# Projection weights' loads begun by ScalarE instead of SyncE, with new places for the work

## The chip, the cores and the metric

The kernel runs on one core of a Trainium2 chip. The metric is the device time of one execution in microseconds; 1185.76 us is the median of three runs of the kernel before. A profiled execution gives, beside the time, a record of every instruction and transfer: TensorE (PE, with its weight loads as PEld), VectorE (DVE), ScalarE (ACT), GpSimd (POOL) and SyncE (SP), which here only starts DMA transfers.

## The reference

One layer over 8 sequences of 256 tokens with 256 features, all in float32. The input is normalized; an attention with 16 heads and a feed-forward part both read the normalized input, and both are added to the input.

```python
xn = _layernorm(x)
q, k = rope(xn @ Wq.T), rope(xn @ Wk.T)            # 16 heads of 128
v, g = xn @ Wv.T, xn @ Wg.T
s = clip(xn @ Ws1.T @ Ws2.T + bs2, -32, 32)        # 64 slots a head
es, enz = exp(s), exp(-cumlogsumexp(s))            # over the tokens
ok = enz * (tril(q @ k.T * scale) @ es)
qv = softmax(ok)
o = tril((qv * enz) @ es.T) @ v
attn = (rmsnorm(o) * g_norm_weight * silu(g)) @ Wo.T
inter = gelu(xn @ Wgate.T) * (xn @ Wup.T)          # 2048 wide, weights from 4-bit codes and scales
out = x + attn + inter @ Wdown.T
```

## The kernel before, in words

The tokens are cut into four groups of 512 (two sequences each), the heads into eight pairs. The attention runs over 32 steps, one for each group and pair of heads; the feed-forward part is cut into small units that are put between the attention's. The program is written out by a planner at build time (`manual_schedule`): it keeps a clock for each engine, estimates when the stages of a chain can run, and so decides in which order the instructions stand in each engine's queue. On the chip each queue runs strictly in that order; semaphores hold an instruction back until its inputs are there.

A loop step n holds the units of several attention steps. `POS` gives each unit's place within the loop step, from 0 to 1; `START` gives other places for the first two loop steps; `FEED` says over which part of a loop step the feed-forward units are spread, `FIRST`, `LAST` how many of them the first and last loop steps get, `DUE` how many pieces of feed-forward weights are to be decoded by each step, and `NORM_AT` where the later groups' normalizations are begun. Where a unit's inputs would be late by the planner's clock, it puts in up to four feed-forward units ahead of it.

The units of an attention step, in the order of the data:

- `rope` (four for a step: q and k of two heads, L637): two matmuls of 512 columns into a bank (L645); ScalarE copies the bank's halves crosswise (L655, L656); VectorE multiplies by the cosines (L658); GpSimd multiplies by the sines and adds (L663, L664).
- `states` (L573): two small matmuls (L584), the clipping (L598), exponentials (L602, L619), prefix sums (L624) and four reciprocals (L630), which make `enz`; `es` is turned by a transposition of blocks (L519), four stores to DRAM (L523), a load back (L532) and a copy (L612).
- `value` and `gate` (two each, L670 and L683, matmuls L706): v is copied (L679), the gate is made of a tanh (L692) and a product (L694).
- `scores` (two, L718): q by k (L725, L728), masked by VectorE (L716).
- `logits` (L736): matmuls L745, product with `enz` (L756), and the way through DRAM as for `es`, to `okT`.
- `softmax` (L769): maxima (L781), exponentials (L792), the same way through DRAM again, and GpSimd's product that makes `prT` (L803).
- `cross` (L811), `weights` (L835, matmuls L845, masked by L855) and `apply` (L872), in the loop step after.
- `outputs` (two, L879, matmuls L888), the normalization and gating (L901, L906, L910, L914), the way through DRAM, and `close` (L929, matmuls L941), which adds two steps' heads to the residual.

The feed-forward units are `ffn_gate` (L437 with L444, L446, L448, L450, L452), `ffn_up` (L466, L475) and `ffn_down` (L491, L409). Their weights are decoded by VectorE (L388, L392, L394). The eight PSUM banks are given out in the order in which the planner expects them to come free; a matmul into a bank waits for the last reader of its former content.

A step's projection weights lie in two tiles, one for q and k (`wts0`) and one for v and the gate (`wts2`), with one buffer each. So a load of the next step's weights must wait until the last matmul has read the old ones. All transfers are started by SyncE, whose queue runs in order: what stands behind a load that waits, waits too. `load_w` (L254) starts a load, and has places of its own, behind the fourth `rope` and the fourth `vg` unit of a loop step:

```python
put("rope", 3, load_w, n + 2, 0)
...
put("vg", 3, load_w, n + 1, 2)
```

Of the kernel before, what the change touches and what calls it, by code (L numbers as in the profile page):

```python
# [34 lines left out]

POS = {'scores': (0.054, 0.064),
 'logits': (0.148,),
 'softmax': (0.335,),
 'cross': (0.146,),
 'weights': (0.169,),  # L40
 'low': (0.1465,),
 'states': (0.167,),
 'outputs': (0.364, 0.453),
 'close': (0.367, 0.61),
 'rope': (0.176, 0.315, 0.368, 0.485),
 'vg': (0.561, 0.79, 0.922, 0.953)}
START = {-1: {'states': (0.575,), 'rope': (0.155, 0.358, 0.421, 0.588)},
 0: {'vg': (0.044, 0.057, 0.103, 0.241),
     'scores': (0.082, 0.162),
     'states': (0.336,),  # L50
     'logits': (0.251,),
     'softmax': (0.433,),
     'rope': (0.238, 0.267, 0.272, 0.485)}}
FEED = {-1: (0.336, 1.0)}
NORMS = {0: 1, 2: 2, 5: 3}
WO = (1, 3, 4, 6)
NORM_AT = (0.204, 0.593)
FIRST = [0.17, 1.57]
LAST = [1.56, 3.5]
DUE = [4, 6, 7, 7, 8, 9, 10, 11, 11, 11, 12, 13, 14, 15, 16, 16, 16, 16, 18, 19, 19, 22, 23, 23, 24]  # L60


@with_exitstack
def layer_kernel(ctx: ExitStack, tc: tile.TileContext, a: dict, out: bass.AP):
# [15 lines left out]
    nc = tc.nc  # L80
# [21 lines left out]
    def V(n):  # L102
        return "v", 0.15 + 0.00105 * n
# [4 lines left out]
    def pe(t):  # L108

        clock["pe"] += t  # L110
# [12 lines left out]
    def advance(until=None):  # L123

        while chains:
            c = min(chains, key=lambda c: (begin(c), c.rank))
            t = begin(c)
            if until is not None and t > until:
                return
            if isinstance(c.what, Chain):  # L130
                c.at = t
            else:
                e, cost, *kb = c.what
                clock[e] = t + cost
                c.at = t + cost + 0.1
                if kb:
                    c.at = lands(clock[e], kb[0])
            c.what = next(c.gen, None)
            if c.what is None:
                chains.remove(c)  # L140
                for users in c.banks:
                    if not any(u in chains for u in users):
                        freed.append(max(u.at for u in users))
            if until is None:
                return
# [4 lines left out]
    asking = [False]  # L150
# [85 lines left out]
    wts = {}  # L236
# [17 lines left out]
    def load_w(n, k):  # L254

        if n < N:
            w = aw.tile([P, 2, 2, 2 * DK], F32, tag=f"wts{k}", name=f"wts{k}")
            nc.sync.dma_start(out=w, in_=a["wqkvg"][steps[n][1]][:, k : k + 2])
            wts[n, k] = w
            loads((n, k), 512)  # L260

# [311 lines left out]
    def states(n):  # L573
# [60 lines left out]
        to["es_at"] = chain(swapped(), es, u)  # L634
        to["states"] = chain(summed(), esT, enz)

    def rope(n, j, which):  # L637

        g, hp = steps[n]
        w = wts[n, 0][:, which, :, j * DK : (j + 1) * DK]  # L640
        need_x(g)
        clock["pe"] = max(clock["pe"], landed[n, 0])
        ps = bank()
        for c in range(2):
            nc.tensor.matmul(  # L645
                ps, lhsT=w[:, c, :], rhs=xT[:, c, g * G : (g + 1) * G], start=c == 0, stop=c == 1
            )
        tag = "qk"[which]
        y = new(p2, [P, 2, T], tag, 2)
        z = new(p2, [P, 2, T], "z", 2)  # L650
        pv = ps.rearrange("p (b t) -> p b t", b=2)

        def work():
            yield "s", 1.16
            nc.scalar.copy(z[0:64], pv[64:128])  # L655
            nc.scalar.copy(z[64:128], pv[0:64])  # L656
            yield V(512)
            nc.vector.tensor_tensor(y, pv, cos_b, ALU.mult)  # L658

        def added():  # L660
            yield first
            yield "g", 2.55
            nc.gpsimd.tensor_tensor(z, z, sin_b, ALU.mult)  # L663
            nc.gpsimd.tensor_tensor(y, y, z, ALU.add)  # L664

        pe(1.72)
        first = chain(work(), ps, y, z)
        of[n][tag, j] = y, chain(added(), y, z)

# [13 lines left out]
    def gate(n, i):  # L683

        to = of[n]
        if i == 0:
            to["sg"] = new(p2, [P, TC, 2 * DK], "sgate")
        s, (pst, ps) = to["sg"][:, i : i + 2, :], vg(n, 1, i)

        def work():  # L690
            yield S(512)
            nc.scalar.activation(s, ps, AF.Tanh, scale=0.5)  # L692
            yield V(512)
            nc.vector.scalar_tensor_tensor(s, s, 1.0, ps, ALU.add, ALU.mult)  # L694

        to["sg", i] = chain(work(), pst, to["sg"])

    def vg(n, which, i):
        g, w = steps[n][0], wts[n, 2]
        need_x(g)  # L700
        pst = bank()
        ps = pst.rearrange("p (i d) -> p i d", i=2)
        for k in range(2):
            tt = slice(g * G + (i + k) * P, g * G + (i + k + 1) * P)
            for c in range(2):
                nc.tensor.matmul(  # L706
                    ps[:, k, :], lhsT=xT[:, c, tt], rhs=w[:, which, c, :],
                    start=c == 0, stop=c == 1,
                )
        pe(1.72)  # L710
        return pst, ps
# [291 lines left out]
    for n in range(-1, N + 1):  # L1003
        at = []
        pos = START.get(n, {})

        def put(name, k, f, *args):
            place = pos.get(name, POS[name])
            at.append((place[k], len(at), f, args))

        def put_at(place, f, *args):
            at.append((place, len(at), f, args))

        def put_norm(g, places):
            for k, h in enumerate((0, 2)):
                put_at(places[k], norm, g, h)

        if n == -1:
            put_norm(0, (0.0, 0.0))
            for h in (0, 2):  # L1020
                put_at(0.1, norm_turn, 0, h)
            put_at(0.2, low_rank, 0)
        if n + 1 < N:
            if n >= 0 and steps[n][1] == 7:
                put("low", 0, low_rank, steps[n][0] + 1)
            put("states", 0, states, n + 1)
            for k, (j, which) in enumerate(((0, 0), (0, 1), (1, 0), (1, 1))):
                put("rope", k, rope, n + 1, j, which)
            put("rope", 3, load_w, n + 2, 0)
        if 0 <= n < N:  # L1030
            for k, (f, i) in enumerate(((value, 0), (value, 2), (gate, 0), (gate, 2))):
                put("vg", k, f, n, i)
            put("vg", 3, load_w, n + 1, 2)
            for j in range(2):
                put("scores", j, scores, n, j)
            put("logits", 0, logits, n)
            put("softmax", 0, softmax, n)
        if n in WO:
            put_at(0.6, load_wo, 4 * WO.index(n))
        gn = NORMS.get(n)  # L1040
        if gn:
            if gn > 1:
                put_at(0.0, load_x, gn * TC, TC)
            put_norm(gn, NORM_AT)
        if n > 0:
            put("cross", 0, cross, n - 1)
            put("weights", 0, weights, n - 1)
            for k in range(2):
                put("outputs", k, outputs, n - 1, k)
            if n % 2 == 1 and n > 1:  # L1050
                for k in range(2):
                    put("close", k, close, n - 2, 2 * k)
            if n == N:
                for k in range(2):
                    put_at(2.0, close, N - 1, 2 * k)
        upto = round(banks * sum(weight[: n + 2]) / sum(weight))
        lo, hi = FEED.get(n, (0.0, 1.0))
        for k in range(upto - fed):
            put_at(lo + (hi - lo) * (k + 0.5) / (upto - fed), feed)
        fed = upto  # L1060
        upto = DUE[n + 1] if n + 1 < len(DUE) else 24
        for k in range(sent, upto):
            put_at((k - sent + 0.3) / (upto - sent), lambda k=k: k < len(parts) or decode_next())
        sent = max(sent, upto)
        for _, _, f, args in sorted(at, key=lambda e: e[:2]):
            while f is close and args == (N - 1, 2) and feeding:
                last, *its = feeding.pop(0)
                last(*its)
            if f is feed:
                ahead = ahead - 1 if ahead > 0 or not feed() else ahead  # L1070
                continue
            while f in UNITS and not ready(f, args):
                if ahead >= AHEAD and n < N or not feed():
                    f(*args)
                    break
                ahead += 1
            if f not in UNITS:
                f(*args)
            advance(clock["pe"])
            while ahead < 0 and feed():  # L1080
                ahead += 1
# [74 lines left out]
```

## Time and profile before

| | |
|---|---|
| median of three runs | 1185.76 us (1185.39 to 1186.27) |
| profiled execution | 1186.14 us |
| its span | 1184.4 us |
| mean granted TensorE clock | 0.997 |
| weight loads (L258) | 64 of 512 KB, median 3.8 us to landing |

The page gives the busy time of each engine as a share of the span. An engine's idle time is put down to what ended it, with total, number and longest of the waits. In timelines a row has its start, its length, the engine, the line, and in brackets the idle time ahead of it. Times count from the span's start.

### The profile page before, as it was taken

How to read it: one execution, taken by the hardware profiler on the slowest of the kernel's cores; microseconds unless marked ns; L12 is line 12 of the kernel's file. 1: busy time of each engine (PE TensorE's matmuls, PEld its weight loads, DVE VectorE, ACT ScalarE, POOL GpSimd, SP SyncE). 2: the span in 40 equal slices, each digit the busy share in tenths (PEclk: the TensorE clock that was granted, in tenths of full speed). 3: DMA queues.
4: the chain of work that ended last, by engine and by line, in shares of the span. 5: the costliest groups of instructions: out<-in, count | busy, mean ns of one | idle time of the engine just before them, and what ended most of it. 6: DMA issues, size and time to landing. Idle time of an engine off the chain costs nothing.

```text
span 1184.4 us, 18121 instructions
## 1 busy us (share of the span) xinstructions
PE 1173.3 (99%) x5830; PEld 828.5 (70%) x5830; DVE 881.3 (74%) x1690; ACT 537.3 (45%) x1685; POOL 490.7 (41%) x439
## 2 busy tenths in 40 slices
PE   9899999999999999999999999999999999999998
PEld 6466676866767777767767677676676677766865
DVE  7978878886676788877587776868777666768553
ACT  4544444554444454443454543535544344555321
POOL 5445435454343444443354443444434334454110
PEclk9999999999999999999999999999999999999999
DMA  5335444454343443343343334334333433432322
GB/s 209 111 106 165 136 124 148 134 143 120 89 134 99 116 135 97 96 117 109 90 143 116 99 112 121 109 106 125 92 97 106 117 103 111 135 98 79 106 58 61
DMA packets 143087, 135.30 MB, mean 114 GB/s; under 512 B 21264, under 2 KB 110480, under 8 KB 142992
## 3 DMA queue, kind: packets, MB, share of 16 engines
q1 hardware_dynamic: 142992, 134.15, 38.7%
q8 instruction: 46, 0.75, 0.3%
q14 instruction: 49, 0.40, 0.1%
HBM read 88.47 MB, written 45.61 MB: 113 GB/s over the span
## 4 chain that ended last, share of the span: by engine, by line
PE 87%; DVE 6%; DMA 2%; SPq 2%; issue 1%; POOL 1%; ACT 1%; DVEq 0%; ACTq 0%; POOLq 0%
PE ps L645 17%; PE ps L706 16%; PE ps L491 9%; PE ps L941 9%; PE ps L466 8%; PE ps L437 8%; PE ps L888 4%; PE ps L725 4%; PE ps L745 3%; PE ps L845 3%; PE ps L728 2%; PE ps L584 1%; PE ps L820 1%; DMA okT<-by_way 1%; SPq L523 1%
## 5 line engine op out<-in xcount | busy, mean ns | idle before, releaser
L663 POOL TENSOR_TENSOR z<-z,turns 128x512 f32<-128x512 f32 x128 | 169.6, 1325 | 226.8 <-ACT z L656 220.7
L645 PE MATMUL ps<-xT,wts 128*128 128x512 f32 x512 | 240.3, 599 | 0.5 <-ACT xT L349 0.5
L706 PEld LDWEIGHTS ps<-wts,xT 128*128 128x128 f32 x1024 | 194.5, 190 | 61.4 <-issue 32.5
L706 PE MATMUL ps<-wts,xT 128*128 128x256 f32 x1024 | 236.5, 379 | 0.0
L645 PEld LDWEIGHTS ps<-xT,wts 128*128 128x128 f32 x512 | 91.0, 190 | 82.9 <-issue 74.8
L437 PE MATMUL ps<-xT,w_gate 128*128 128x512 f32 x256 | 120.8, 594 | 0.2 <-DVE at L716 0.2
L466 PE MATMUL ps<-xT,w_up 128*128 128x512 f32 x256 | 120.7, 594 | 0.0
L630 DVE RECIPROCAL enz<-enz 128x128 f32<-128x128 f32 x128 | 118.4, 933 | 0.0
L491 PE MATMUL ps<-w_down,inter 128*128 128x256 f32 x512 | 115.7, 380 | 0.0
L941 PE MATMUL ps<-w_o,ogT 128*128 128x256 f32 x496 | 112.1, 379 | 0.0
L655 ACT COPY z<-ps 64x512 f32<-64x512 f32 x128 | 74.5, 582 | 82.3 <-PE ps L645 67.3
L491 PEld LDWEIGHTS ps<-w_down,inter 128*128 128x128 f32 x512 | 96.3, 190 | 16.3 <-issue 4.0
L446 POOL TENSOR_SCALAR t<-t 128x512 f32<-128x512 f32 x64 | 39.7, 621 | 150.3 <-ACT t L444 147.7
L803 POOL TENSOR_TENSOR prT<-okT,enz 128x512 f32<-128x512 f32 x32 | 40.6, 1269 | 148.2 <-DMA okT<-by_way 141.8
L941 PEld LDWEIGHTS ps<-w_o,ogT 128*128 128x128 f32 x496 | 93.1, 190 | 12.5 <-issue 0.5
L664 POOL TENSOR_TENSOR q<-q,z 128x512 f32<-128x512 f32 x64 | 84.1, 1315 | 34.3 <-DVE q L658 31.0
L664 POOL TENSOR_TENSOR k<-k,z 128x512 f32<-128x512 f32 x64 | 82.1, 1282 | 30.8 <-DVE k L658 13.2
L409 DVE TENSOR_TENSOR res<-ps,res 128x512 f32<-128x512 f32 x63 | 42.6, 679 | 68.9 <-PE ps L491 42.4
L910 POOL TENSOR_TENSOR ss<-ss,nhalf 128x4 f32<-128x4 f32 x64 | 65.6, 1025 | 59.8 <-DVE ss L906 59.0
L792 ACT ACTIVATE ok<-okT,mx 128x64 f32<-128x64 f32 x256 | 85.6, 337 | 10.0 <-DVE mx L786 9.3
L444 ACT ACTIVATE t<-ps 128x512 f32<-128x512 f32 x64 | 38.1, 596 | 109.2 <-PE ps L437 109.1
L448 DVE TENSOR_TENSOR t<-ps,t 128x512 f32<-128x512 f32 x64 | 43.4, 680 | 58.2 <-POOL t L446 58.0
(83 smaller groups left out, 1934.3 us busy)
## 6 DMA issues: line engine op xcount, KB each, us to landing
wts<-in_wqkvg_dram SPq DMA_DIRECT2D x64, 512.0 KB, 3.8
by_way<-ok SPq DMA_DIRECT2D x256, 64.0 KB, 1.8
okT<-by_way SPq DMA_DIRECT2D x64, 256.0 KB, 2.8
by_way<-og SPq DMA_DIRECT2D x256, 64.0 KB, 1.8
ogT<-by_way SPq DMA_DIRECT2D x64, 256.0 KB, 2.9
by_way<-u SPq DMA_DIRECT2D x128, 64.0 KB, 1.8
u<-by_way SPq DMA_DIRECT2D x32, 256.0 KB, 2.8
pk<-in_codes_dram SPq DMA_DIRECT2D x12, 256.0 KB, 3.7
```

Source lines behind the costliest of these rows:

```text
L437: nc.tensor.matmul(pg, lhsT=w_gate[:, c, ns], rhs=xT[:, c, gs], start=c == 0, stop=c == 1)
L466: nc.tensor.matmul(pu, lhsT=w_up[:, c, ns], rhs=xT[:, c, gs], start=c == 0, stop=c == 1)
L491: nc.tensor.matmul(ps[:, k, :], lhsT=inter[g, n][0][:, (i + k) * P : (i + k + 1) * P], rhs=w_dn[:, n, :], start=n == 2 * q, stop=n == 2 * ...
L630: nc.vector.reciprocal(r, r)
L645: nc.tensor.matmul(ps, lhsT=w[:, c, :], rhs=xT[:, c, g * G : (g + 1) * G], start=c == 0, stop=c == 1)
L655: nc.scalar.copy(z[0:64], pv[64:128])
L663: nc.gpsimd.tensor_tensor(z, z, sin_b, ALU.mult)
L664: nc.gpsimd.tensor_tensor(y, y, z, ALU.add)
L706: nc.tensor.matmul(ps[:, k, :], lhsT=xT[:, c, tt], rhs=w[:, which, c, :], start=c == 0, stop=c == 1,)
L792: nc.scalar.activation(pr[:, js, i, :], okT[:, js, i, :], AF.Exp, bias=mx[:, k : k + 1], scale=SCALE, accum_out=sm[:, k : k + 1],)
L910: nc.gpsimd.tensor_tensor(ss, ss, nhalf, ALU.pow)
L941: nc.tensor.matmul(ps[:, k, :], lhsT=ogT[hh][0][:, i + k], rhs=w_o[:, (hp // 2) * 4 + hh, :], start=hh == 0, stop=hh == 3,)
```

## The change

The loads for the first two steps stay where they were. From the third step on a load is started by ScalarE, in the middle of the stages of the last unit that reads the old weights: behind the second crosswise copy of the fourth `rope` for q and k, and behind the tanh of the second `gate` unit for v and the gate. As a load is now begun by a stage of a chain, and not by a unit, the new function `given` makes the planner advance its chains until the load has been begun, before a unit reads the new tile. Places of `softmax`, `outputs`, `close`, `rope` and `vg` are changed, and several for the first two loop steps; the shares of feed-forward units in the first and last loop steps, one place of the normalizations and two entries of `DUE` are changed too.

```diff
- 'softmax': (0.335,),
+ 'softmax': (0.267,),
- 'outputs': (0.364, 0.453),
- 'close': (0.367, 0.61),
- 'rope': (0.176, 0.315, 0.368, 0.485),
- 'vg': (0.561, 0.79, 0.922, 0.953)}
-START = {-1: {'states': (0.575,), 'rope': (0.155, 0.358, 0.421, 0.588)},
+ 'outputs': (0.307, 0.396),
+ 'close': (0.433, 0.61),
+ 'rope': (0.179, 0.318, 0.371, 0.488),
+ 'vg': (0.622, 0.79, 0.922, 0.953)}
+START = {-1: {'states': (0.575,), 'rope': (0.155, 0.358, 0.421, 0.543)},
-     'states': (0.336,),
-     'logits': (0.251,),
-     'softmax': (0.433,),
+     'states': (0.262,),
+     'logits': (0.241,),
+     'softmax': (0.437,),
-FEED = {-1: (0.336, 1.0)}
+FEED = {-1: (0.156, 1.0)}
-NORM_AT = (0.204, 0.593)
-FIRST = [0.17, 1.57]
-LAST = [1.56, 3.5]
-DUE = [4, 6, 7, 7, 8, 9, 10, 11, 11, 11, 12, 13, 14, 15, 16, 16, 16, 16, 18, 19, 19, 22, 23, 23, 24]
+NORM_AT = (0.291, 0.593)
+FIRST = [0.06, 1.57]
+LAST = [1.53, 3.5]
+DUE = [4, 6, 7, 7, 8, 9, 10, 11, 11, 11, 12, 13, 14, 15, 16, 16, 16, 16, 18, 18, 19, 22, 23, 24, 24]
...
-            nc.sync.dma_start(out=w, in_=a["wqkvg"][steps[n][1]][:, k : k + 2])
+            (nc.scalar if n > 1 else nc.sync).dma_start(out=w, in_=a["wqkvg"][steps[n][1]][:, k : k + 2])
...
+    def given(n, k):
+        if asking[0] and (n, k) not in wts:
+            raise Late
+        while (n, k) not in wts:
+            advance()
...
     def rope(n, j, which):
         g, hp = steps[n]
+        given(n, 0)
...
             nc.scalar.copy(z[64:128], pv[0:64])
+            if (j, which) == (1, 1) and n:
+                load_w(n + 1, 0)
...
             nc.scalar.activation(s, ps, AF.Tanh, scale=0.5)
+            if i == 2 and n:
+                load_w(n + 1, 2)
...
     def vg(n, which, i):
+        given(n, 2)
...
-            put("rope", 3, load_w, n + 2, 0)
+            if n == -1:
+                put("rope", 3, load_w, 1, 0)
...
-            put("vg", 3, load_w, n + 1, 2)
+            if n == 0:
+                put("vg", 3, load_w, 1, 2)
```

## The prediction

> **What bounds the kernel now.** I read the page first, then the table by windows, then the waits of TensorE and SyncE, then the timelines of the first 70 us. The page and the windows:
>
> ```profile
> span 1184.4 us, 18121 instructions
> PE 1173.3 (99%) x5830; PEld 828.5 (70%) x5830; DVE 881.3 (74%) x1690; ACT 537.3 (45%) x1685; POOL 490.7 (41%) x439
> ```
>
> ```profile
> 30.00:60.00 30.00, 25.15 (x83) 13.36 (x83) 29.09 (x61) 15.60 (x38) 13.89 (x13) 0.94 0.40 113
> 60.00:100.00 40.00, 40.00 (x229) 28.89 (x229) 30.34 (x57) 16.62 (x53) 17.48 (x15) 0.96 0.48 139
> 350.00:450.00 100.00, 100.00 (x513) 72.33 (x512) 77.24 (x147) 44.07 (x145) 40.41 (x36) 1.00 0.38 109
> ```
>
> After the stretch's length come busy time of PE, PEld, DVE, ACT, POOL, then the granted clock. From 60 us on TensorE has no idle left: no change there can win anything but the few tenths of small waits. The one hole is in 30 to 60: 4.85 us idle, and a clock under 1. The waits name it, and the wait that the change takes away:
>
> ```profile
> PE ps L725 <- POOL k L664: 4.8, 1, 4.8
> POOL prT L803 <- DMA okT<-by_way: 141.8, 28, 9.6
> ```
>
> ```profile
> SPq L258 <- PE ps L645: 137.7, 27, 7.9
> SPq L258 <- PE ps L706: 44.6, 22, 9.0
> ```
>
> SyncE stands 182 us before weight loads, and what is queued behind (the stores and loads of the transpositions) stands with it; but TensorE waits for a transposition only through prT, in tenths. The hole itself, on TensorE, then VectorE, then GpSimd:
>
> ```profile
> 52.30 0.38 PE L728 MATMUL ps<-q,k 128*128 128x128 f32 x2
> 57.54 1.22 PE L725 MATMUL ps<-q,k 128*128 128x256 f32 x2 [4.85 <-POOL k L664]
> 64.22 3.72 PE L491 MATMUL ps<-w_down,inter 128*128 128x256 f32 x16
> 67.87 1.16 PE L845 MATMUL ps<-prT,esT 64*128 64x128 f32 x16
> ```
>
> ```profile
> 12.29 1.56 DVE L388 TENSOR_SCALAR u<-pk 128x256 int32<-128x256 int32 x2
> 55.40 0.67 DVE L658 TENSOR_TENSOR k<-ps,turns 128x512 f32<-128x512 f32 x1
> 56.66 0.70 DVE L519 STREAM_TRANSPOSE ok<-ok 128x512 f32<-128x512 f32 x1
> ```
>
> ```profile
> 12.38 1.33 POOL L663 TENSOR_TENSOR z<-z,turns 128x512 f32<-128x512 f32 x1 [5.19 <-DVE w_gate L394]
> 64.95 1.26 POOL L803 TENSOR_TENSOR prT<-okT,enz 128x512 f32<-128x512 f32 x1 [7.47 <-DMA okT<-by_way]
> ```
>
> TensorE comes to the second scores of step 1 at 52.5 and gets their k at 57.5, because VectorE, busy without a break from 10.7 to 62, made it only at 55.4. The hole costs 5.0 us. In windows of 1 us the clock is 0.63 in 56 to 57, 0.50 from 57 to 63 and 0.95 in 63 to 64: about 6.8 us at half speed, 3.4 us lost. So 8.4 us is the most that can be won here.
>
> **The change, part by part.**
>
> *The loads.* 60 of the 64 move from SyncE to ScalarE, 0.34 us each (median of L258): 20.5 us more for an engine busy 537 of 1184. On ScalarE a load stands behind the stage that reads the old weights' last bank, so the wait for TensorE is over by then. What it still waits for is the transfer eight places earlier in the program, whose semaphore it takes again. For the q/k loads that is mostly a store of u; in before it landed 4.2 to 12.5 us ahead of that stage's end in all later steps: 0. For the v/gate loads it is mostly a store of ok, which landed between 1.8 us after the stage and 9.7 us before. So ScalarE may stand 1.8 us, before the stages of the next bank; TensorE uses the gate that comes from there 10 us of its own work later: 0 either way. The weights are used 19 to 25 us after the old ones (PE work between, by the order), and land in 3.8 us: 0. Shorter waits on SyncE shorten logits to prT (26.7 to 35.7 us in before against 31 to 41 to the weights stage): that is slack, and the small waits for it (0.3 at 340, 0.3 at 762) go, with some of the four other waits under half a microsecond: -0.5, between 0 and -1.2.
>
> *The opening.* The order shows the same TensorE units up to states of step 2, except that the w_down unit (3.46 us) now comes after the first weights stage. So the first weights stage breaks even at 67.87 - 3.46 = 64.41. It waits for prT, prT for the transposition of ok, and that for VectorE's queue. Counted up to that transposition, VectorE has one L448, L452 and L475 fewer (0.6 each from start to start), two L716 (0.43 each), one set of norm statistics (1.3) and L306 (0.1), and one L392 and L394 more (0.45, 0.62): -3.0 us, from 56.66 to 53.7. The 0.6 us that it idles at 47.2 falls away. New idle: the states stage now stands behind the fourth rope, so L598 can't start before 18.1 (+0.46), and the copy of es now stands ahead of the copies of v and of L444 on ScalarE; u takes 7.2 us from its transposition to that copy (20.42 to 27.58), so L448 comes 1.1 us late. That gives 54.7, if VectorE and GpSimd meet as often as before.
>
> They meet in L388, L392, L394 and L624: the pair of L388 takes 0.49 us at 10.69 and 1.56 at 12.29 beside GpSimd's z. In before the starts show 6.5 us lost so up to 56.66. Walking the new order with the rows' durations, and VectorE losing every close meeting, gives 9.4; with the close ones split, 8.2; the least, with only those that no order avoids, 4. I take 8.2: 56.3. [...]
>
> Then 0.65 for the transposition, 6.5 for the way through DRAM (6.3 to 6.9 where nothing stands between; 7.6 in before, as the stores of z stood ahead of okT, and now stand behind), 1.35 for prT: 64.8, +0.4. Ends: 52.1 + 0.65 + 6.3 + 1.35 = 60.4 (-4.0), and 57.5 + 0.65 + 7.6 + 1.35 = 67.1 (+2.7). TensorE's idle time is then spread: about 2.5 us at 27.5 (the bank for the L466 unit is freed by the first L716, now behind all four reciprocals), 1.6 near 52, 2.4 near 55, 1 near 59, 2 before the weights. No single gap is as long as the 5 us that brought the half clock, so I price the clock at 0; were it to come again at one of them, +3.4, of which the waits behind it hide most.
>
> *The places after that.* Outputs stand one rope earlier: in 22 of 32 steps one rope lies between weights and the first outputs, in before in one. At 517 to 521 the weights end at 519.03 and the first L855 ends at 521.07, 2.04 later, in 20 of 32 steps so; with one rope TensorE comes at 2.2. The margin of 0.1 is less than the 0.43 by which a weight load runs ahead (31.13 to 31.56). Where a weight came just in time (29.74) the unit took 0.1 longer. 21 steps at 0.06: +1.2, between 0 and 21 x 0.2 = 4.2. Softmax, close and vg move by 2 us at most against slacks of 4 us and more: 0.
>
> *The tail.* The order of the last 25 us is the same: 0.
>
> **Sum.** +0.4 + 1.2 - 0.5 = +1.1. On the profiled execution's 1186.14 (span 1184.4 and 1.74 around it), which lies 0.38 above the median of 1185.76: 1186.9 as a median. I count 0.2% (2.4 us) as what a measurement can tell from no change.
>
> [...]
>
> **The rivals.**
>
> 1. *The opening closes (faster).* VectorE and GpSimd meet little, prT comes at 60.4: -4.0 and -0.5, 1181.3. For: VectorE has 3 us less ahead of prT. Against: L388, L392 and L394 stand closer together, while GpSimd works on the ropes. It decides from prT's stage at 62.0 on downwards. Chance 0.23.
>
> 2. *The outputs wait (slower).* The first L855 comes after TensorE in the 21 steps, 0.2 each: +4.2, with the opening's +0.4 and the -0.5: 1189.9. For: a margin of 0.1 us. Against: the same stages stand ahead of L855 as before. It decides from 0.12 us a step on. With it I count an opening at its bad end (+2.7). Chance 0.29.
>
> 3. *The move does nothing for the transpositions.* SyncE stands at the stores of ok instead, which wait for VectorE; the way through DRAM stays 7.6: +1.1 more, 1188.0. It lies within the forecast's own range.
>
> **How the numbers follow.** Forecast, with rival 3: 0.48, 1183.4 to 1188.1, likeliest 1186.9. Faster by over 0.2%: 0.23; slower: 0.29. The range leaves out the outermost tenth at each end: 1182.0 (the opening near its good end) to 1190.2 (rival 2 with a slow way through DRAM).
>
> **What would show it.** On SyncE L258 is left with 4 loads and no wait worth a microsecond; ScalarE issues 60. In windows TensorE's idle time within 25 to 66 us is several gaps of 1 to 3 us, the clock stays 1.00, and the first weights stage starts near 64.8. VectorE idles near 18 and 34. L888's waits for L855 are many and short. From 100 us on TensorE is again at 100%. I am wrong if the gap at 27.5 or at 55 is above 3.5 us and halves the clock, if VectorE reaches the transposition of ok before 54, or if a stage that I priced at 0 (the v/gate load on ScalarE, close) shows as a wait of TensorE.

## The result, and the profile after

The changed kernel takes 1189.39 us (median of 12 runs, 1185.88 to 1191.33); the kernel before took 1185.43 us beside it (12 runs, 1184.11 to 1187.47). The ratio is 1.0029, with a 95% interval of 1.0022 to 1.0037: slower by 2.6 to 4.4 us. That lies inside the predicted range (1182.0 to 1190.2), but not in its likeliest case: the forecast was 1186.9 us and no measurable change (0.48), and the change costs 0.29%, which had a chance of 0.29.

The profiled execution took 1187.73 us and had no half clock. Ten of the twelve runs had a mean granted clock below 1.000 and took 1188.57 to 1191.33 us; the two others took 1187.73 and 1185.88. So the profile shows one of the two better executions, and part of the loss is not in it. (The profile of one experiment, `e2_loads`, fell on an execution at a clock of 0.95 throughout; it is not read, and that run is left out of the kernel's median below.)

The page of the changed kernel, and its windows (length, then busy time of PE, PEld, DVE, ACT, POOL, then the granted clock):

```profile
span 1185.9 us, 18113 instructions
PE 1171.3 (99%) x5830; PEld 827.3 (70%) x5830; DVE 891.7 (75%) x1690; ACT 538.0 (45%) x1685; POOL 493.6 (42%) x439
```

```profile
30.00:60.00 30.00, 25.42 (x84) 12.98 (x85) 28.61 (x54) 15.49 (x39) 13.87 (x12) 1.00 0.45 132
60.00:100.00 40.00, 37.79 (x224) 28.04 (x224) 34.12 (x67) 18.10 (x56) 18.09 (x16) 1.00 0.49 140
350.00:450.00 100.00, 100.00 (x517) 72.67 (x516) 79.86 (x148) 44.91 (x142) 43.06 (x37) 1.00 0.40 116
```

From 350 to 450 us nothing has changed for TensorE: it is busy all the time. In the opening the clock is whole in this execution, but TensorE stands 4.6 us between 30 and 60 as before (4.85), and 2.2 us more behind 60. The waits of the changed kernel (total, times, longest), of TensorE, GpSimd and SyncE:

```profile
PE ps L466 <- DVE at L730: 3.2, 1, 3.2
PE ps L739 <- DVE t L452: 2.3, 1, 2.3
PE ps L859 <- POOL prT L817: 1.3, 1, 1.3
...
PE ps L834 <- DVE at L730: 0.9, 1, 0.9
PE ps L437 <- DVE sgate L707: 0.7, 1, 0.7
...
PE ps L902 <- DVE wt L869: 0.3, 1, 0.3
```

```profile
POOL prT L817 <- DMA okT<-by_way: 84.1, 23, 9.7
```

```profile
SPq L523 <- DVE ok L519: 301.4, 46, 15.2
...
SPq L258 <- PE ps L720: 6.5, 1, 6.5
```

(The lines of the code have moved: L645, L716, L725, L803, L845, L855, L888 of before are now L654, L730, L739, L817, L859, L869, L902.) The change does what it says: SyncE's 182 us ahead of weight loads are gone, it now stands at the stores of ok, which wait for VectorE, and GpSimd waits 84 us for okT where it waited 142. But TensorE had no use for that. Its one hole of 4.85 us has become a row of smaller ones. On TensorE, then on VectorE:

```profile
28.29 0.38 PE L742 MATMUL ps<-q,k 128*128 128x128 f32 x2
31.92 1.98 PE L466 MATMUL ps<-xT,w_up 128*128 128x512 f32 x4 [3.24 <-DVE at L730]
...
59.29 0.67 PE L739 MATMUL ps<-q,k 128*128 128x256 f32 x2 [2.27 <-DVE t L452]
...
66.08 1.16 PE L859 MATMUL ps<-prT,esT 64*128 64x128 f32 x16 [1.27 <-POOL prT L817]
```

```profile
12.21 1.57 DVE L388 TENSOR_SCALAR u<-pk 128x256 int32<-128x256 int32 x2 [4.27 <-DMA pk<-in_codes_dram]
...
28.10 3.35 DVE L630 RECIPROCAL enz<-enz 128x128 f32<-128x128 f32 x4
31.38 1.88 DVE L730 TENSOR_TENSOR at<-ps,mask 128x384 f32<-128x384 f32 x4
...
57.87 0.70 DVE L519 STREAM_TRANSPOSE ok<-ok 128x512 f32<-128x512 f32 x1
```

The bank of the L466 unit is freed by the first L730, and that stands behind four reciprocals in one piece. VectorE's whole queue is late, too: its first codes landed at 12.21 us, against 10.69 in the profile of before.

To see where the time goes I subtract, from the start of each matmul, the full-clock duration of all the matmuls ahead of it. What is left is TensorE's lost time so far, and the order of the units does not disturb it. (The durations are means by line and shape from one profile; only differences between kernels are read.) Against the profile of before, in us:

| kernel, one profiled execution of each | at 75 us | at 1175 us | mean granted clock |
|---|---|---|---|
| before | 0 | 0 | 0.997 |
| after | +2.0 | +1.6 | 1.000 |
| e5_all_places | +3.3 | +3.7 | 0.999 |
| e1_opening | +2.7 | +7.4 | 0.997 |
| e4_old_opening | +2.1 | +2.2 | 0.997 |
| e9_loads_again | +0.6 | +1.5 | 0.997 |
| e10_qk_only | -0.9 | -1.2 | 0.999 |
| e11_vg_only | -0.1 | +1.9 | 0.999 |
| e6_keep_clock | +5.3 | +4.2 | 0.997 |
| e12_after_clock | +3.3 | +2.9 | 1.000 |
| e7_before_clock | -0.9 | -2.1 | 1.000 |
| e8_codes_first | -1.1 | -1.6 | 0.999 |

The changed kernel loses its time in the opening. Behind it, it wins back 1.6 us between 100 and 200 us, where before had small waits, and loses 1.2 us later in several places; the longest wait there is 0.7 us at a gate unit at 755 us (the L437 line above). Matmuls that an experiment adds count as lost time in this table.

### The profile page after: what moved, and what is told of

Read it like the earlier page. It is cut to its first block, busy times and chain, and to the rows that moved or that the text cites. A ratio compares the mean times of both kernels' runs of the same rounds, so it can differ in the third digit from the quotient of the medians.

```text
span 1185.9 us, 18113 instructions
## 1 busy us (share of the span) xinstructions
PE 1171.3 (99%) x5830; PEld 827.3 (70%) x5830; DVE 891.7 (75%) x1690; ACT 538.0 (45%) x1685; POOL 493.6 (42%) x439
## 4 chain that ended last, share of the span: by engine, by line
PE 94%; DVE 5%; issue 1%; ACT 0%; POOL 0%; DVEq 0%; POOLq 0%; ACTq 0%
PE ps L654 18%; PE ps L720 18%; PE ps L491 9%; PE ps L955 9%; PE ps L466 9%; PE ps L437 9%; PE ps L902 5%; PE ps L739 4%; PE ps L759 3%; PE ps L859 3%; PE ps L742 2%; PE ps L584 2%; PE ps L834 1%; PE ps L886 1%; DVE enz L630 1%
## 5 line engine op out<-in xcount | busy, mean ns | idle before, releaser
L654 PE MATMUL ps<-xT,wts 128*128 128x512 f32 x512 | 238.7, 599 | 0.5 <-ACT xT L349 0.5
L654 PEld LDWEIGHTS ps<-xT,wts 128*128 128x128 f32 x512 | 91.0, 190 | 83.7 <-issue 77.5
L466 PE MATMUL ps<-xT,w_up 128*128 128x512 f32 x256 | 121.0, 595 | 3.6 <-DVE at L730 3.2
L437 PE MATMUL ps<-xT,w_gate 128*128 128x512 f32 x256 | 120.7, 594 | 0.7 <-DVE sgate L707 0.7
L902 PEld LDWEIGHTS ps<-v,wt 128*128 128x128 f32 x512 | 65.8, 191 | 29.0 <-issue 15.1
L703 ACT ACTIVATE sgate<-ps 128x512 f32<-128x512 f32 x64 | 38.1, 596 | 95.2 <-PE ps L720 89.3
```

What stands on the lines that cost most here:

```text
L437: nc.tensor.matmul(pg, lhsT=w_gate[:, c, ns], rhs=xT[:, c, gs], start=c == 0, stop=c == 1)
L466: nc.tensor.matmul(pu, lhsT=w_up[:, c, ns], rhs=xT[:, c, gs], start=c == 0, stop=c == 1)
L654: nc.tensor.matmul(ps, lhsT=w[:, c, :], rhs=xT[:, c, g * G : (g + 1) * G], start=c == 0, stop=c == 1)
L902: nc.tensor.matmul(po[:, i, :], lhsT=wt[:, i, :], rhs=v[:, i, j * DK : (j + 1) * DK], start=False, stop=i == TC - 1,)
```

## Experiments

### Which part of the change costs: places, loads, or outputs

Theory 1: the opening's places cost all. Theory 2: the loads on ScalarE do. Theory 3: the outputs one rope earlier do. Four kernels, each with a part of the change.

`e1_opening`, the kernel before with the opening's constants of the change:

```diff
-START = {-1: {'states': (0.575,), 'rope': (0.155, 0.358, 0.421, 0.588)},
+START = {-1: {'states': (0.575,), 'rope': (0.155, 0.358, 0.421, 0.543)},
...
-FEED = {-1: (0.336, 1.0)}
+FEED = {-1: (0.156, 1.0)}
-NORM_AT = (0.204, 0.593)
-FIRST = [0.17, 1.57]
...
+NORM_AT = (0.291, 0.593)
+FIRST = [0.06, 1.57]
...
```

> The kernel before with the opening's places alone (START, FEED, FIRST, LAST, NORM_AT, DUE as after the change); POS and the loads' engine stay as before. Medians so far: before 1185.4, after 1189.4. Theory 1, the opening costs all: about 1189, with the first weights stage near 66 against a break-even of 64.4 (+1.7), and in most runs a mean clock of 0.997 to 0.999, the half clock coming on top. Theory 2, the loads on ScalarE cost it: 1185 to 1186. Theory 3, the outputs one rope earlier cost it: 1185 to 1186 as well.

`e5_all_places`, the same with `POS` of the change as well, so the whole change without its loads:

```diff
- 'softmax': (0.335,),
+ 'softmax': (0.267,),
...
- 'outputs': (0.364, 0.453),
+ 'outputs': (0.307, 0.396),
...
```

> All places as after the change, but the loads begun by SyncE at the places of before: the change without its loads. Theory 1, the opening: 1189 to 1190. Theory 2, the loads: 1185 to 1186. Theory 3, outputs one rope earlier: 1188 to 1190, with L888 waiting for L855 in some 21 steps. If the loads' move is what makes the new places possible at all, then slower than 1190, by waits for the transpositions behind SyncE's waits (0.3 to 1 us in several steps).

`e4_old_opening`, the changed kernel with START, FEED, NORM_AT, FIRST, LAST and DUE of before:

```diff
...
-FEED = {-1: (0.156, 1.0)}
+FEED = {-1: (0.336, 1.0)}
...
-NORM_AT = (0.291, 0.593)
-FIRST = [0.06, 1.57]
...
+NORM_AT = (0.204, 0.593)
+FIRST = [0.17, 1.57]
...
```

> The changed kernel with the opening's places of before (START, FEED, FIRST, LAST, NORM_AT, DUE); the loads on ScalarE and POS stay changed. Theory 1, the opening costs all: 1185 to 1186, the hole of 5 us at the second scores and its half clock back as in before. Theory 2 or 3, loads or outputs: 1188 to 1189.5, with waits of TensorE between 100 and 1150 us that the kernel before does not have.

`e2_loads`, the loads' code of the change with every place as before:

```diff
-            nc.sync.dma_start(out=w, in_=a["wqkvg"][steps[n][1]][:, k : k + 2])
+            (nc.scalar if n > 1 else nc.sync).dma_start(out=w, in_=a["wqkvg"][steps[n][1]][:, k : k + 2])
...
```

> The changed code of the loads with every place as before: 60 of 64 weight loads on ScalarE behind their stage, nothing else. Theory 1, the opening costs all: 1185 to 1186, with the small waits for the transpositions gone (-0.5). Theory 2, the loads on ScalarE cost it: 1188 to 1189.5, and then TensorE's waits name a stage of ScalarE or a late load. Theory 3: 1185 to 1186.

| kernel | median us | ratio to before | 95% interval |
|---|---|---|---|
| e1_opening | 1192.60 | 1.0052 | 1.0038 to 1.0066 |
| e5_all_places | 1189.89 | 1.0032 | 1.0021 to 1.0042 |
| e4_old_opening | 1187.40 | 1.0011 | 1.0002 to 1.0019 |
| e2_loads | 1187.07 | 1.0011 | 1.0002 to 1.0020 |

The places alone give the whole of the change's cost (1.0032 against 1.0029), with the loads where they were. With the old opening some two thirds of it go. Theory 3 falls by the waits: it wanted many short ones of L902 for L869, some 0.2 us in each of 21 steps, and there is one of 0.3 us in the profiles of after and of e5. (In e4's there are two, 0.9 us at 73.2 and 0.3. That e4 and e2 cost the same settles nothing, as the moved loads have a cost of their own with e2's places, shown below.) Theory 1 carries most, but not all: neither kernel with moved loads came out at 1185 to 1186, as theory 1 wanted. And the opening's places without the new `POS` cost 6 us, more than theory 1 said, since TensorE then also waits for a transposition near 104 us, which brings the half clock once more:

```profile
PE ps L845 <- POOL prT L803: 3.7, 3, 2.3
```

So the new places behind the opening take away what the new opening costs there: in the table above e1 loses 4.7 us behind 75 us, e5 0.4. In e5 the profile has the half clock that the profile of the changed kernel has not:

```profile
31.59 3.32 PE L466 MATMUL ps<-xT,w_up 128*128 128x512 f32 x4 [3.25 <-DVE at L716]
34.70 2.29 PE L645 MATMUL ps<-xT,wts 128*128 128x512 f32 x4
```

Four matmuls of 512 columns in 3.32 us instead of 1.98, behind the same hole. The second ok is then transposed at 59.11, and in e1, with the same half clock, at 58.59; in the three profiles of this opening without it that was 57.87, 56.78 and 57.14, though VectorE began earlier in e5 and e1 (11.89 and 11.39 us) than in after (12.21). VectorE idles 1.5 us ahead of an L452 at 38.9 and 38.4 us in these two and not in the three others. That fits a chain made late by the half clock, and the table at 75 us has +3.3 and +2.7 for the two against +2.0.

### Is it the half clock?

`e6_keep_clock` fills two holes of the changed kernel's opening, 3.24 us at 28.7 and 2.27 us at 57.0, with 9 and 5 matmuls (128x128) that nobody reads, written into columns of a score bank that are not used:

```diff
...
+    keep = lambda c: [nc.tensor.matmul(last[-1][:, T + P :], lhsT=ones, rhs=ones, start=True, stop=True) for _ in range(c)]
...
+        keep(5 if (n, j) == (1, 1) else 0)
...
-        pe(1.3)
+        pe(1.3); keep(9 if (n, j) == (0, 1) else 0)
...
```

> [...] Theory A, the half clock that comes in 10 of 12 runs after these holes is what most of the difference is: the mean clock is 1.000 in every run, and the median falls from 1189.4 to about 1186.8, where the two runs of the changed kernel without half clock lay (1187.7, 1185.9). Theory B, the waits behind the holes hide the half clock: clock 1.000 too, but 1189 as before.

Measured: 1189.38 us, 1.0027 [1.0016, 1.0037], and a mean clock below 1.000 in six of eight runs. Theory A as put there falls: the clock didn't stay up. The profile names the place, a third hole, ahead of the first weights stage. SyncE, then TensorE:

```profile
57.57 1.81 SPq L523 DMA_DIRECT2D by_way<-ok  x4
63.07 0.34 SPq L532 DMA_DIRECT2D okT<-by_way  x1
```

```profile
67.18 2.08 PE L859 MATMUL ps<-prT,esT 64*128 64x128 f32 x16 [3.45 <-POOL prT L817]
```

VectorE was 1.1 us earlier than in the changed kernel's profile (ok at 56.78), but the stores took so long that prT came 1.1 us later. Still, the two runs at clock 1.000 took 1186.98 and 1187.32 us, the six others 1188.72 to 1190.35. So I filled the third hole too.

`e12_after_clock`, with the lines of e6 and this one:

```diff
-        pss = [bank(), bank()]
+        pss = [bank(), bank()]; last.append(pss[1]); keep(8 if n == 0 else 0)
```

> The changed kernel with matmuls nobody reads in all three holes of its opening: 9 and 5 as in e6_keep_clock and 8 more (1.7 us) between the states and the first weights stage, where e6_keep_clock waited 3.4 us for prT and then ran 6.8 us at half clock. Theory A in its second form, the half clock behind any of the three holes is what separates the changed kernel's runs: clock 1.000 in at least four of five runs and a median of about 1187, as in the four runs of after and e6_keep_clock without half clock (1187.7, 1185.9, 1187.0, 1187.3), plus up to 0.5 where the matmuls outlast the hole. If something else separates them: 1189 again at clock 1.000.

Measured: clock 1.000 in all eleven runs, but 1188.59 us, 1.0024 [1.0015, 1.0032]. The clock is mended, and about 0.6 us are won, by the intervals perhaps nothing. By this run the half clock is not most of what separates the changed kernel from before. The profile says where the gain went:

```profile
67.72 1.16 PE L859 MATMUL ps<-prT,esT 64*128 64x128 f32 x16 [1.66 <-POOL prT L817]
```

The first weights stage comes 1.6 us later than in the changed kernel's profile, though VectorE transposed ok 0.7 us earlier (57.14). The transfers from 57 to 64 us, with the median time from issue to landing, in e12 and then in the changed kernel:

```profile
q8 instruction: 1, 0.02, 1.5%
...
by_way<-ok SPq DMA_DIRECT2D x4, 64.0 KB, 4.6
```

```profile
by_way<-ok SPq DMA_DIRECT2D x4, 64.0 KB, 2.4
```

In e12 a packet of 16 KB of instructions falls into the stores of ok (at 60.10 us, taking 1.69; 1.5% of 16 engines times 7 us); the stores land at 62.85 to 63.35, while nearly nothing else is moved. In e6 such a packet is at 59.75 (1.74 us), with the same effect. In the changed kernel's profile it is at 64.17 (0.88 us), in the last half microsecond of okT's load, and the stores land in 2.4 us. The traces of the 13 profiles that are read bear this out: the stores of ok behind whose start such a packet begins within 1.5 us land in a median of 3.0 us (251 stores), the others in 1.75 (3077); for the loads of okT it is 3.7 us (27) against 2.7 (805). Added matmuls shift the packet: in the kernel before it is at 62.21, within okT's load, which takes 3.55 us; in `e7_before_clock` below it is at 55.24, and the load takes 2.6. It was not moved alone in any run. So the test of the clock has a cost of its own, and the share of the clock stays open. The difference of the two ratios (e12 against after) gives 0.6 us. The distance between the runs with and without half clock gives 2.9 us in the changed kernel (1189.7 against 1186.8, means of ten and two runs), 2.5 in e6 (1189.6 against 1187.2, six and two runs), 2.2 in e1 and 0.4 in e5 (one run at clock 1.000 each); as those runs may differ in more than the clock, this is no proof.

### What the half clock costs the kernel before

`e7_before_clock` fills the old hole in the same way (`keep` as above):

```diff
...
+            last.append(ps); keep(16 if (n, j, b) == (1, 1, 0) else 0)
```

> The kernel before with 16 such matmuls (3.4 us) in its hole of 4.85 us at 52.7 to 57.5, behind which its clock is halved in every run. Theory A as the prediction priced it (6.8 us at half clock cost 3.4 us): about 1182.5. Theory B, part of it is hidden because the third and fourth mask product of VectorE end at 61.25 whatever the clock: gain 0.9 to 1.5, about 1184.5 to 1185.

```profile
53.35 3.74 PE L717 MATMUL ps<-mask 128*128 128x128 f32 x32
58.13 0.70 PE L725 MATMUL ps<-q,k 128*128 128x256 f32 x2 [1.04 <-POOL k L664]
...
60.12 1.59 PE L745 MATMUL ps<-at,es 128*64 128x256 f32 x10
61.90 0.86 PE L745 MATMUL ps<-at,es 128*64 128x256 f32 x6 [0.19 <-DVE at L716]
62.70 0.70 PE L584 MATMUL ps<-rT,w_s 64*128 64x256 f32 x4
...
66.98 1.16 PE L845 MATMUL ps<-prT,esT 64*128 64x128 f32 x16
```

Measured: 1184.08 us, 0.9986 [0.9978, 0.9995], clock 1.000 in all eleven runs, and a spread of 1.5 us instead of 2.5. It is the fastest kernel here, ahead of before and of the changed kernel. Theory B holds, with a gain a little above the 0.9 to 1.5 us it named: the hole stays, the half clock goes, and that is worth 1.7 us (0.6 to 2.6 by the interval) and not the 3.4 that the prediction gave it. The rows show what hides the rest: from the first logits matmul to the next unit it is now 2.6 us, against 1.4 at 516 us in the kernel before, as TensorE comes to the masks of VectorE (L716) too early.

### Do the codes' landings set the opening?

`e8_codes_first` sends the first codes and scales ahead of the small weights and tables:

```diff
-    load_w(0, 0)
+    load_w(0, 0); first = new(de, [P, 512], "pk", 3, I32), new(de, [P, 512], "sc", 3)
+    [nc.sync.dma_start(out=t, in_=a[k][0]) for t, k in zip(first, ("codes", "scales"))]
...
```

> The kernel before with the first codes and scales (0.5 MB) sent ahead of small, turns and w_s, in place of behind them: VectorE's first L388 started between 10.7 and 12.2 us in the six profiles so far, after 2.7 to 4.3 us of idle time, and should start near 9 to 9.5. Theory C, VectorE's queue sets the opening and the landing of the codes sets VectorE's: all of the gain of 1.5 to 2.5 us arrives, 1183.5 to 1184.5, and the hole at the second scores shrinks by as much. Rival: q's first product waits for turns instead (L658 at 13.8 or later as before), gain 0 to 0.5, 1185.5 to 1186.

Measured: 1184.98 us, 0.9993 [0.9984, 1.0002]. The first codes land early, but VectorE then stands at the second ones:

```profile
8.83 0.49 DVE L388 TENSOR_SCALAR u<-pk 128x256 int32<-128x256 int32 x2 [1.00 <-DMA pk<-in_codes_dram]
...
12.80 1.05 DVE L388 TENSOR_SCALAR u<-pk 128x256 int32<-128x256 int32 x2 [2.29 <-DMA pk<-in_codes_dram]
```

From 13.78 on its queue runs as in the profile of before, to 0.02 us, and the hole at the second scores is as long as ever (4.83). So theory C falls in this form: what one landing gives, the next takes. The middle of the interval is a gain of 0.8 us; it isn't shown, as the interval reaches past 1.

`e13_best` puts e7 and e8 together, with both of the diffs above.

> The kernel before with both changes that gained: 16 matmuls in its hole (1184.1 alone) and the first codes sent first (1185.0 alone, 0.7 under before). If the gains add, 1183.4; if the codes only shortened what the half clock made long, 1184.1. Clock 1.000 in every run.

Measured: 1184.58 us, 0.9992 [0.9983, 1.0001], no better than e7 alone. Nine of eleven runs kept the clock (mean 1184.4); two had the half clock. In one of them, the profiled one, TensorE waited far behind the opening for a transposition that came late, and got it there (the other has no profile):

```profile
761.36 1.88 PE L845 MATMUL ps<-prT,esT 64*128 64x128 f32 x16 [2.55 <-POOL prT L803]
```

### What the moved loads cost by themselves

`e9_loads_again` is e2 once more:

> The loads on ScalarE with all places as before, again, for an undisturbed profile and a narrower interval: the first time gave 1.0011 [1.0002, 1.0020]. If the move itself costs, 1187 again and a wait of TensorE or a later start of a stage in the steady part, against the kernel before, of about 1 us in all; if that was chance or a late landing of the codes, 1186, and the time from the first weights stage to the end the same as in before (1116.5 us).

Measured: 1187.52 us, 1.0019 [1.0011, 1.0028]. The cost is there again. In its profile TensorE waits 0.67 us for prT at 100.2, and 0.42 for a bank behind it, in the step in which the v/gate load is started on ScalarE half a microsecond ahead of okT's load. So one half of the move each, with all places as before:

`e10_qk_only`, set against the kernel before; as in the next diff, the line that starts the loads is shown, and the places of the moved loads are in the part left out:

```diff
-            (nc.scalar if n > 1 else nc.sync).dma_start(out=w, in_=a["wqkvg"][steps[n][1]][:, k : k + 2])
+            (nc.scalar if n > 1 and k == 0 else nc.sync).dma_start(out=w, in_=a["wqkvg"][steps[n][1]][:, k : k + 2])
...
```

> All places as before; only the q/k loads are begun by ScalarE, the v/gate loads stay on SyncE. With both loads moved the kernel takes 1187.5 (ratio 1.0019 [1.0011, 1.0028]), and the trace shows the v/gate load of step 2 at 92.95 us, 0.5 us ahead of the load of okT on SyncE at 93.43; okT then took 5.5 us to prT, where in the kernel before it took 3.0 with that load behind it at 94.20. Theory D, this collision is the cost of the moved loads: without it 1185.7 to 1186.2, and okT to prT near 3.0 there. Rival, ScalarE's time for the issues or an order of the planner: half of it, about 1186.7.

`e11_vg_only`, against the kernel before as well:

```diff
-            (nc.scalar if n > 1 else nc.sync).dma_start(out=w, in_=a["wqkvg"][steps[n][1]][:, k : k + 2])
+            (nc.scalar if n > 1 and k == 2 else nc.sync).dma_start(out=w, in_=a["wqkvg"][steps[n][1]][:, k : k + 2])
...
```

> The other half: only the v/gate loads on ScalarE, the q/k loads on SyncE, all places as before. Theory D, the collision with okT in step 1 to 2: 1187.0 to 1187.5, with the wait of TensorE for prT (about 0.8 us) near 99 us and okT to prT above 5 us. Rival, ScalarE's time or the planner: about 1186.7.

Measured: q/k alone 1185.13 us, 0.9996 [0.9988, 1.0005]; v/gate alone 1188.26 us, 1.0023 [1.0014, 1.0032], a little above theory D's range. The rival, half the cost each, falls, and theory D holds: by the table of lost time e11 loses 2.0 us between 75 us and the end, and 1.6 us of that are waits of TensorE at 100 to 102.5, for prT (1.17) and for a bank behind it (0.42); e10 loses none. First e10: SyncE's queue and GpSimd; then e11: ScalarE's queue, SyncE's, GpSimd and TensorE.

```profile
91.92 0.36 SPq L532 DMA_DIRECT2D okT<-by_way  x1
92.33 0.46 SPq L258 DMA_DIRECT2D wts<-in_wqkvg_dram  x1
...
94.78 1.28 POOL L817 TENSOR_TENSOR prT<-okT,enz 128x512 f32<-128x512 f32 x1 [2.91 <-DMA okT<-by_way]
```

```profile
92.28 0.39 ACTq L258 DMA_DIRECT2D wts<-in_wqkvg_dram  x1
...
93.33 0.38 SPq L532 DMA_DIRECT2D okT<-by_way  x1
...
98.76 1.26 POOL L817 TENSOR_TENSOR prT<-okT,enz 128x512 f32<-128x512 f32 x1 [6.02 <-DMA okT<-by_way]
...
100.07 1.16 PE L859 MATMUL ps<-prT,esT 64*128 64x128 f32 x16 [1.17 <-POOL prT L817]
```

Where the 512 KB start behind okT's load, prT follows that load by 2.9 us; where they start 1.05 us ahead of it, by 5.4. SyncE's queue had kept okT in front, because the weight load stood in the same queue behind it. Such meetings are not rare: okT's load has a weight load started less than 2 us ahead of it 12 times in the kernel before (median 4.4 us to landing, 2.7 for the other 52) and 5 times in e11. Only the one at 93 us makes TensorE wait in e11.

In the changed kernel the new places keep this from happening there: okT's load is at 90.36 us, 2.1 us ahead of the weights' at 92.45, and prT starts at 93.29. That fits the runs, in which the loads add nothing to the cost of the places (after 1.0029, e5 1.0032).

## Why the prediction was right and where it was wrong

- **The loads, 0.** Right for the changed kernel, and by luck, since the step "0 either way" looked only at who waits for the loads and when they are needed. It left out what half a megabyte does to a transposition that it overtakes. With the old places that costs 2.3 us by the ratio (e9), all of it from the v/gate loads (e11); with the new places it isn't there.
- **The opening, +0.4.** Mis-sized: in the profile, which has no half clock, it is +2.0 us by the table at 75 us. The walk along VectorE's queue held, to within half a microsecond if the start is allowed for: ok was foreseen at 56.3 and came at 57.87, and VectorE was 1.5 us late from its first codes on. (The ends, 52.1 and 57.5, are the same walk with 4 and 9.4 us lost in place of 8.2.) The way from there to prT was foreseen at 7.15 us (0.65 and 6.5) and took 6.9. (Without the 0.65 that is 6.2 us, against 7.6 in before, and not only because the stores of z no longer stand ahead of okT: okT's load itself took 2.6 us, and 3.55 in before, where an instruction packet fell into it.)
- **VectorE's start.** What was missing is that this start is not fixed: in ten of the eleven profiles read that have the old order of the first loads VectorE began between 11.2 and 12.3 us, and the profile of before, from which I summed, was the earliest of all with 10.69. But the start is no part of the change, and a late one comes with the old opening too: in e11 VectorE began at 12.27 us and transposed ok at 57.78. At like starts the two openings reach that point together, where the prediction had the new one 0.4 us ahead. Yet e11 stands at -0.1 at 75 us, with a mean granted clock of 0.999 where before has 0.997. So the late start by itself does not explain the +2.0; how much of it is the start and how much the new order stays open.
- **The holes.** Predicted 2.5 at 27.5, 1.6 near 52, 2.4 near 55, 1 near 59 and 2 ahead of the weights; measured 3.24 at 28.7, 0.4 at 54.7, 2.27 at 57.0, 0.9 at 60.9 and 1.27. The places are right, and the cause of the first, the only one given; the sum is near (9.5 against 8.1), though the second hole is a quarter of what was foreseen.
- **The clock, priced at 0.** This is the reasoning that failed outright: "No single gap is as long as the 5 us that brought the half clock." I took one gap that did it for the length that is needed. Ten of twelve runs had a clock below 1.000, and the profiles of e1 and e5 show the half clock right behind the hole of 3.25 us. The condition that I set for being wrong, a gap above 3.5 us, was set too high for the same reason.
- **What the half clock is worth.** "6.8 us at half speed, 3.4 us lost" and "8.4 us is the most that can be won" were sums over TensorE alone, and they count 1.3 us twice: the half clock began at 56.27 us, the hole ended at 57.54. In the 5.55 us of work at half clock 2.8 us were lost. With the half clock gone and the hole kept, before gains 1.7 us (e7): for the rest TensorE waits for VectorE's masks, which make its logits unit 1.2 us longer than in the steady part.
- **Outputs one rope earlier, +1.2.** Not there: L902 waits for L869 once, 0.3 us, as in before. The margin of 0.1 us was enough in the 21 steps. (In e4, which keeps the old opening, one wait of 0.9 us at 73.2 is added.)
- **Small waits, -0.5.** Right in sum: -1.6 between 100 and 200 us and +1.2 behind that.
- **The rivals.** The first didn't come about (prT's stage started at 64.76, where it had to be under 62.0 to decide). The second gives nearly the measured time, 1189.9, but its mechanism is not what happened. The third is refuted by the way through DRAM in the opening, 6.2 us where it had 7.6, and by GpSimd's waits for okT: 84.1 us against 141.8 in before, and 103.3 with the places alone (e5).
- **The range.** That 1189.39 lies in it is luck. Its upper end was set by rival 2's waits and a slow way through DRAM, and neither came; what came instead, the longer opening and the half clock, had +0.4 and 0.
- **The signs.** SyncE has 4 loads left and ScalarE 60 as foreseen. Three of the four still wait, 6.5, 5.2 and 1.7 us, where nothing above a microsecond was foreseen, at no cost to TensorE. VectorE's idle time near 18 and 34 didn't come. The v/gate load on ScalarE, named as what would prove me wrong, isn't a wait in the changed kernel.

Against the kernel before the changed kernel's median is 4.0 us up in its own comparison (3.4 by the ratio). The places cause it (e5). 1.6 us stand in the two profiles, of which one began VectorE's work early and the other late. Runs sorted by their clock put 0.4 to 2.9 us on the half clock behind the new holes; e12, which keeps the clock whole, wins 0.6. How the cost divides between the holes and the clock stays open. The way through DRAM took 9 us in e6 and e12 with an instruction packet in the stores of ok; the traces show that such stores land later, but no run moved the packet alone.

## What to carry to other kernels

Moving a transfer to another engine's queue also changes what it overtakes (in e11 prT came 5.4 us behind okT's load, in e10 2.9): look for the small transfer that used to stand in front of it in the steps where somebody waits for it, and test each moved load by itself. A hole of TensorE costs more than its length when the clock is cut behind it (in before 1.7 us more, by e7), so look at several runs' mean clocks, and not at one profile; a few matmuls that nobody reads can cost less than the clock that they keep (e7, 0.9986), but they also shift what stands behind them (in e12 the first weights stage came 1.6 us later). When one long hole is broken into short ones, look at the clock behind each of them as well: it was halved behind holes of 3.25 us (e1, e5) and of 2.35 (e1).

## What was not expected of the hardware

The clock was also halved behind holes shorter than the 4.85 us of before, and the length of a hole alone did not tell whether it would be. Some of TensorE's holes in the profiles, with the clock behind them, which the length of the next matmuls shows:

| kernel | idle, us | until | behind it |
|---|---|---|---|
| before | 4.85 | 57.54 | half clock (0.50) from 56.27 to 63.10 us |
| after | 3.24 | 31.92 | full: four L466 in 1.98 us |
| after | 2.27 | 59.29 | full: two L739 in 0.67 us |
| e5_all_places | 3.25 | 31.59 | half: four L466 in 3.32 us |
| e1_opening | 3.25 | 31.07 | half: four L466 in 3.08 us |
| e1_opening | 2.14 | 60.01 | full: two L725 in 0.67 us |
| e1_opening | 2.35 | 105.95 | half: eight L872 in 1.07 us, against 0.61 at full clock |
| e6_keep_clock | 3.45 | 67.18 | half: sixteen L859 in 2.08 us, against 1.16 |
| e12_after_clock | 1.66 | 67.72 | full: sixteen L859 in 1.16 us |
| e13_best | 2.55 | 761.36 | half: sixteen L845 in 1.88 us, against 1.16 |

One hole of the new opening, 3.24 us in one profile and 3.25 in two, had the full clock behind it once and the half clock twice. The runs show the same: of the 24 runs of after, e1 and e5, which share this hole, four had a mean clock of 1.000. With the hole of 4.85 us all 86 runs of before in the experiments had a clock below 1.000; with 1.04 us left of it, in e7, all eleven had 1.000. What decides between full and half clock behind a hole is not shown: no run moved a hole without changing anything else.
